# The last rows of a two-layer graph kernel: multiply ahead of the norm, maximum with a negated offset, loads ahead, two store queues

## The chip, the cores and the metric

The kernel runs on one core of a Trainium2 chip. The metric is device time in microseconds, the median of several executions. The span that a profile shows is 1.8 us shorter than the time of the same execution. The profile of the kernel before is of an execution of 2804.74 us, slower than the three timed ones.

In this kernel TensorE does the matmuls, with results in tiles of the memory PSUM; VectorE and ScalarE work on tiles in PSUM or in the other on-chip memory, SBUF, and GpSimd on tiles in SBUF. DMA transfers (loads and stores) are issued from the queues of SyncE and ScalarE, those of the last block before the change all from SyncE. The residual is the `x` that the last step adds.

## The reference, cut to what matters

```python
def _layer_norm(z, a, b, eps=0.001):
    mu = jnp.mean(z, axis=-1, keepdims=True)
    sigma = jnp.std(z, axis=-1, keepdims=True, ddof=1)
    return (z - mu) / (sigma + eps) * a + b
...
for l in range(L):                                  # two layers
    ...                                             # scores, masked exp, attention
    h_lin = jnp.einsum('bsh,oh->bso', h, W_lin[l]) + b_lin[l]
    ctx = jnp.matmul(attention, h_lin)
    h = jax.nn.relu(_layer_norm(ctx, ln_a[l], ln_b[l]))
...
x = x + h                                           # out: 128 x 64 x 768, fp32
```

The mean is already gone in the kernel (the weights are centred), so the norm of a row is one sum of squares. In the data `ln_a` is one and `ln_b` is zero, but the kernel computes both.

## The kernel before

The second layer's second pass goes through 16 blocks `u` of 512 tokens. In the last block it works in two halves `r` of two tiles `k`, 128 rows each. `linear` forms `hl` with 15 groups of matmuls per half, which share the PSUM banks X, Y, Z and V; after each group ScalarE and VectorE add its result into `hl` (`read`). `context` multiplies the attention with `hl` into PSUM tiles `aux`. `finish` does norm, relu and residual:

```python
def finish(u, r):
    cx = context(u, r)
    ...
    for k in range(2):                                              # ScalarE
        nc.scalar.activation(zs[k], cx[k], AF.Square, accum_out=ss[:, k:k + 1])
    nc.scalar.activation(sd, ss, AF.Sqrt, bias=floor, scale=1.0 / (H - 1.0))
    def inverse():                                                  # VectorE
        nc.vector.tensor_scalar_add(rs, sd, EPS_LN)
        nc.vector.reciprocal(rs, rs)
    def scaled(k):
        nc.vector.scalar_tensor_tensor(zs[k], cx[k], rs[:, k:k + 1], rows["a"], op0=ALU.mult, op1=ALU.mult)
        nc.gpsimd.tensor_add(zs[k], zs[k], rows["b"])               # GpSimd
    def done(k):
        nc.vector.scalar_tensor_tensor(xs[k], zs[k], 0.0, xs[k], op0=ALU.max, op1=ALU.add)
        for h in range(PAIR):
            nc.sync.dma_start(out[...], xs[k][h * S:(h + 1) * S])
        if k and (u < NB - 1 or r == 0):
            residual(u + r, 1 - r)                                  # loads the next xs
    return [inverse, scaled(0), scaled(1), done(0), done(1)]        # as closures (cut)
...
linear(u, (0,), 0, {0: ((u - 1, 0), (12, 13, 15, 19, 21)),
                    11: ((u - 1, 1), (34, 35, 36, 42, 44))}, (1,))
linear(u, (1,), 30, {4: ((u, 0), (50, 51, 52, 56, 58))}, ())
for f in finish(u, 1):
    f()
```

The last lines say after which matmul group of the half (0, 11, 4) the earlier rows' context is formed, and in which slots (two per group) its five steps are issued. The trace shows VectorE's instructions in the order of issue: the outputs of slots 56 and 58 start at 2785.10 and 2787.03 us, the sums of Z and V issued behind them at 2786.70 and 2787.90.

## Time and profile before

| what | value | where from |
|---|---|---|
| time | 2802.02 us median of 3 (2799.44 to 2802.55) | runs |
| span, TensorE busy | 2803.0 us, 98% | page |
| last block's first Z matmul to the end | 49.16 us | trace, 2753.80 to 2802.97 |
| of it: to the end of the last sum into `hl` ("E") | 34.51 us | trace |
| from E to the last output add | 9.93 us | trace |
| from the last add to the end | 4.72 us | trace |

TensorE, 98% busy and 94% of the chain on the page, bounds everything up to the last block. After the last V matmuls nothing is left for it but the context, and the end is a chain through VectorE, TensorE, ScalarE, VectorE, GpSimd, VectorE and the stores. The prediction shows that chain line by line. In the lines of a timeline, the columns are start and length in us, engine, line, operation, output<-inputs, shapes and count; in brackets stands the idle time of the engine before it and what ended it. The lengths of neighbours overlap a little.

### The profile page before, as it was taken

How to read it: one execution, taken by the hardware profiler on the slowest of the kernel's cores; microseconds unless marked ns; L12 is line 12 of the kernel's file. 1: busy time of each engine (PE TensorE's matmuls, PEld its weight loads, DVE VectorE, ACT ScalarE, POOL GpSimd, SP SyncE). 2: the span in 40 equal slices, each digit the busy share in tenths (PEclk: the TensorE clock that was granted, in tenths of full speed). 3: DMA queues.
4: the chain of work that ended last, by engine and by line, in shares of the span. 5: the costliest groups of instructions: out<-in, count | busy, mean ns of one | idle time of the engine just before them, and what ended most of it. 6: DMA issues, size and time to landing. Idle time of an engine off the chain costs nothing.

```text
span 2803.0 us, 46102 instructions
## 1 busy us (share of the span) xinstructions
PE 2755.9 (98%) x18712; PEld 2342.4 (84%) x18712; DVE 1340.9 (48%) x2223; ACT 838.7 (30%) x1452; POOL 1190.1 (42%) x935
## 2 busy tenths in 40 slices
PE   7999999999999999999999999999999999999997
PEld 6788888888888888888788888888888888888885
DVE  6454554454544332232345434443444335666666
ACT  2123222322131244444522221212122214545443
POOL 3343333222322556555333353223222335887875
PEclk9999999999999999999999999999999999999999
DMA  5633343234322243343563432343234204555654
GB/s 155 164 78 74 94 115 87 74 88 119 88 74 76 98 141 117 106 130 106 149 160 97 120 79 74 91 119 85 74 85 118 69 25 145 162 169 158 184 162 125
DMA packets 234068, 310.80 MB, mean 111 GB/s; under 512 B 54144, under 2 KB 184448, under 8 KB 225664
## 3 DMA queue, kind: packets, MB, share of 16 engines
q1 hardware_dynamic: 233568, 307.06, 40.0%
q8 instruction: 149, 2.44, 0.4%
q10 hardware_dynamic: 288, 0.79, 0.1%
q14 instruction: 63, 0.52, 0.1%
HBM read 202.91 MB, written 104.86 MB: 110 GB/s over the span
## 4 chain that ended last, share of the span: by engine, by line
PE 94%; DVE 2%; DMA 1%; ACT 1%; issue 1%; SPq 0%; POOL 0%; DVEq 0%; ACTq 0%; POOLq 0%
PE X L366 23%; PE V L366 15%; PE X L637 12%; PE Y L366 11%; PE Z L366 8%; PE V L637 8%; PE Y L637 6%; PE aux L392 5%; PE Z L637 4%; PE aux L564 3%; DVE m L144 1%; DMA ht<-h 0%; DMA h<-xb 0%; ACT ht L255 0%; DVE w_l L144 0%
## 5 line engine op out<-in xcount | busy, mean ns | idle before, releaser
L144 POOL TENSOR_TENSOR ts<-ht 128x512 f32<-128x512 f32 x441 | 585.7, 1340 | 1242.1 <-DMA ht<-h 555.7
L189 ACT ACTIVATE m<-X 128x512 f32<-128x512 f32 x256 | 152.7, 596 | 1117.1 <-PE X L366 589.5
L144 POOL TENSOR_TENSOR ts<-ht,ts 128x512 f32<-128x512 f32 x189 | 248.9, 1325 | 152.8 <-PE X L637 75.9
L144 DVE TENSOR_TENSOR m<-m,V 128x512 f32<-128x512 f32 x256 | 174.4, 681 | 271.9 <-PE V L366 271.9
L144 DVE TENSOR_TENSOR m<-m,X 128x512 f32<-128x512 f32 x256 | 163.8, 682 | 250.2 <-PE X L366 249.5
L366 PE MATMUL X<-ts,w_l 128*128 128x256 f32 x1024 | 246.6, 384 | 6.0 <-DVE w_l L144 2.1
L637 PE MATMUL X<-w_n,ts 128*128 128x256 f32 x1024 | 244.2, 380 | 0.9 <-ACT hl L189 0.6
L366 PE MATMUL X<-ts,w_r 128*128 128x256 f32 x1024 | 242.1, 379 | 0.2 <-ACT m L189 0.2
L144 DVE TENSOR_TENSOR m<-m,Z 128x512 f32<-128x512 f32 x128 | 88.0, 688 | 318.3 <-ACT m L189 257.3
L366 PEld LDWEIGHTS X<-ts,w_l 128*128 128x128 f32 x1024 | 194.2, 192 | 38.5 <-DVE m L144 4.6
L637 PEld LDWEIGHTS X<-w_n,ts 128*128 128x128 f32 x1024 | 191.6, 190 | 32.2 <-DVE hl L144 2.3
L366 PEld LDWEIGHTS X<-ts,w_r 128*128 128x128 f32 x1024 | 192.2, 190 | 29.6 <-ACT m L189 0.6
L255 ACT ACTIVATE ht<-ht,b_col,a_col 128x512 f32<-128x512 f32 x192 | 144.1, 808 | 142.9 <-DMA ht<-h 142.9
L637 PE MATMUL Y<-w_n,ts 128*128 128x256 f32 x768 | 182.4, 379 | 0.0
L366 PE MATMUL Y<-ts,w_l 128*128 128x256 f32 x768 | 181.8, 380 | 0.0
L366 PE MATMUL Y<-ts,w_r 128*128 128x256 f32 x768 | 181.4, 379 | 0.0
L189 ACT ACTIVATE hl<-X 128x512 f32<-128x512 f32 (+1 forms) x136 | 77.9, 573 | 329.4 <-PE X L637 320.0
L366 PEld LDWEIGHTS Y<-ts,w_l 128*128 128x128 f32 x768 | 146.4, 191 | 20.0
L637 PEld LDWEIGHTS Y<-w_n,ts 128*128 128x128 f32 x768 | 145.9, 190 | 19.8
L366 PEld LDWEIGHTS Y<-ts,w_r 128*128 128x128 f32 x768 | 145.9, 190 | 19.8
L603 POOL TENSOR_TENSOR z<-z,b 128x768 f32<-128x768 f32 x64 | 115.4, 1816 | 94.9 <-DVE z L600 94.9
L144 DVE TENSOR_TENSOR hl<-hl,X 128x512 f32<-128x512 f32 (+1 forms) x136 | 83.1, 653 | 147.2 <-PE X L637 139.8
(106 smaller groups left out, 4684.8 us busy)
## 6 DMA issues: line engine op xcount, KB each, us to landing
ht<-h SPq DMA_DIRECT2D x63, 1536.0 KB, 7.2
h<-xb SPq DMA_DIRECT2D x124, 384.0 KB, 6.8
z<-z SPq DMA_DIRECT2D x128, 192.0 KB, 2.9
x<-z SPq DMA_DIRECT2D x128, 192.0 KB, 8.4
xr<-in_x_dram SPq DMA_DIRECT2D x128, 192.0 KB, 3.7
out_dram<-xr SPq DMA_DIRECT2D x128, 192.0 KB, 2.6
x<-in_x_dram SPq DMA_DIRECT2D x120, 192.0 KB, 8.4
adj<-in_adj_dram SPq DMA_DIRECT2D x64, 128.0 KB, 2.8
```

The lines of the kernel that those rows point to most:

```text
L144: (eng.tensor_add if sign == "+" else eng.tensor_sub)(o, a, b)
L189: nc.scalar.activation(to(o), p, AF.Copy, scale=1.0 if sign == "+" else -1.0)
L255: nc.scalar.activation(ht, ht, AF.Relu, bias=cols[1][:, c:c + 1], scale=cols[0][:, c:c + 1])
L366: nc.tensor.matmul(p[:, g], w[ORDER[i][0]][:, c, g * P:(g + 1) * P], b()[t][:, c, :], start=(new and g == c == 0), stop=(c == K2 - 1), ski ...
L392: nc.tensor.matmul(p[h * S + e:h * S + e + 32, q, e:e + 96], ht[:, c, b * S + e:b * S + e + 32], mb[:, e:e + 96], start=(c == 0), stop=(c ...
L564: nc.tensor.matmul(cx[k][i, m, :HH], at[j, q, :], hl[j, q, m * HH:(m + 1) * HH], start=True, stop=True)
L603: nc.gpsimd.tensor_add(zs[k], zs[k], rows["b"])
L637: nc.tensor.matmul(p[:, n], b[t][:, c, r * P:(r + 1) * P], w[s][:, c, :], start=(i in FIRST and i not in PRELOAD and n == c == 0), stop=(c ...
```

## The change

The intent is to shorten the chain after the last matmuls: load residuals earlier, keep VectorE free for the last sums, multiply by `a` before the root is known, replace GpSimd's add and the relu by a maximum (`max(z + b, 0) + x = max(z, -b) + (x + b)`, with `x + b` made ahead), and store through two queues. In the diffs here some reshapes of tiles are left out.

```diff
+            def last_block(u):
+                rest = big.tile([P, C, T], F32, name="ht").rearrange("p c t -> p (c t)")
+                rows["-b"] = sp.tile([P, H], F32, name="nb", bufs=1)
+                ...                                    # XS[u, r]: four slices of rest; load(r): four DMAs
+                put(1, lambda: load(1))
+                put(6, lambda: nc.gpsimd.tensor_scalar_mul(rows["-b"], rows["b"], -1.0))
+                put(20, lambda: load(0))
+                for xs, slot in zip(XS[u, 1], (22, 40)):
+                    put(slot, lambda xs=xs: nc.gpsimd.tensor_add(xs, xs, rows["b"]))
+
+            def finish_last(u, r):
+                ...
+                for k in (1, 0):
+                    nc.scalar.activation(squares[:, k], cx[k], AF.Square, accum_out=ss[k])
+                    nc.vector.tensor_tensor(zs[1 - k], cx[1 - k], rows["a"], op=ALU.mult)
+                    nc.scalar.activation(rs[k], ss[k], AF.Sqrt, bias=floor, scale=1.0 / (H - 1.0))
+                for k in (1, 0):
+                    nc.vector.tensor_scalar_add(rs[k], rs[k], EPS_LN)
+                    nc.vector.reciprocal(rs[k], rs[k])
+                    nc.vector.scalar_tensor_tensor(zs[k], zs[k], rs[k], rows["-b"], op0=ALU.mult, op1=ALU.max)
+                    nc.vector.tensor_add(xs[k], xs[k], zs[k])
+                    for h, queue in enumerate((nc.sync, nc.scalar)):
+                        queue.dma_start(out[u * NBB + batch(r, k, h)], xs[k][h * S:(h + 1) * S])
...
-                        if k and (u < NB - 1 or r == 0):
+                        if k and u + r < NB - 1:
...
-                    linear(u, (0,), 0, {0: ..., 11: ((u - 1, 1), (34, 35, 36, 42, 44))}, (1,))
-                    linear(u, (1,), 30, {4: ((u, 0), (50, 51, 52, 56, 58))}, ())
+                    # in the last layer:
+                    linear(u, (0,), 0, {0: ..., 9: ((u - 1, 1), (28, 29, 30, 39, 41))}, (1,))
+                    linear(u, (1,), 30, {2: ((u, 0), (44, 45, 47, 61, 62))}, ())
-                    for f in finish(u, 1):
+                    for f in (finish_last if last else finish)(u, 1):
```

More of the change, by code (lines that the diff above doesn't have):

```diff
@@ L571, in pass_two, with load @@
             XS = {}
+            def last_block(u):
+                rest = big.tile([P, C, T], F32, name="ht").rearrange("p c t -> p (c t)")
+                rows["-b"] = sp.tile([P, H], F32, name="nb", bufs=1)
+                for r in range(2):
+                    XS[u, r] = [rest[:, n * H:(n + 1) * H] for n in (2 * r, 2 * r + 1)]
+                def load(r):
+                    for k in range(2):
+                        for h in range(PAIR):
+                            nc.sync.dma_start(XS[u, r][k][h * S:(h + 1) * S], x[u * NBB + batch(r, k, h)])
+                put(1, lambda: load(1))
[4 more added lines that the diff above has]
+            def finish_last(u, r):
+                cx = context(u, r)
+                zs = [sp.tile([P, H], F32, name="z", bufs=4) for _ in range(2)]
+                squares = sp.tile([P, Q, H], F32, name="hl", bufs=2)
+                two = "p (n d) -> p n d"
+                xs = XS[u, r]
+                ss = [stat.tile([P, 1], F32, name="ss_e", bufs=2) for _ in range(2)]
+                rs = [stat.tile([P, 1], F32, name="sd_e", bufs=2) for _ in range(2)]
+                for k in (1, 0):
+                    nc.scalar.activation(squares[:, k].rearrange(two, n=2), cx[k], AF.Square, accum_out=ss[k])
+                    nc.vector.tensor_tensor(zs[1 - k].rearrange(two, n=2), cx[1 - k],
+                                            rows["a"].rearrange(two, n=2), op=ALU.mult)
+                    nc.scalar.activation(rs[k], ss[k], AF.Sqrt, bias=floor, scale=1.0 / (H - 1.0))
[6 more added lines that the diff above has]
+                        queue.dma_start(out[u * NBB + batch(r, k, h)], xs[k][h * S:(h + 1) * S])
+                return []
             def residual(u, r):
@@ L676, in pass_two @@
                         put_sums_t((1, 1, 0), 38, 2, 30)
-                    linear(u, (0,), 0, {0: ((u - 1, 0), (12, 13, 15, 19, 21)),
-                                        11: ((u - 1, 1), (34, 35, 36, 42, 44))}, (1,))
-                    linear(u, (1,), 30, {4: ((u, 0), (50, 51, 52, 56, 58))}, ())
+                        ends = ({0: ((u - 1, 0), (12, 13, 15, 19, 21)), 11: ((u - 1, 1), (34, 35, 36, 42, 44))},
+                                {4: ((u, 0), (50, 51, 52, 56, 58))})
+                    else:
+                        last_block(u)
+                        ends = ({0: ((u - 1, 0), (12, 13, 15, 19, 21)), 9: ((u - 1, 1), (28, 29, 30, 39, 41))},
+                                {2: ((u, 0), (44, 45, 47, 61, 62))})
+                    linear(u, (0,), 0, ends[0], (1,))
+                    linear(u, (1,), 30, ends[1], ())
                     for n in sorted(plan):
                         run(n)
-                    for f in finish(u, 1):
+                    for f in (finish_last if last else finish)(u, 1):
                         f()
```

## The prediction

> **What bounds the kernel now.** I read the page's busy shares and its chain of waits first.
>
> ```profile
> PE 2755.9 (98%) x18712; PEld 2342.4 (84%) x18712; DVE 1340.9 (48%) x2223; ACT 838.7 (30%) x1452; POOL 1190.1 (42%) x935
> ...
> PE 94%; DVE 2%; DMA 1%; ACT 1%; issue 1%; SPq 0%; POOL 0%; DVEq 0%; ACTq 0%; POOLq 0%
> ```
>
> TensorE carries 94% of the chain, and the diff touches no matmul. What it touches is the last of 16 blocks of the second layer, some 50 us of 2803, and within these the stretch after the last matmuls. So I read the timeline of the last 23 us next (start us, us, engine, line, operation, count, then idle time before and its releaser).
>
> ```profile
> 2781.24 1.94 DVE L600 SCALAR_TENSOR_TENSOR z<-aux,rs,a 128x768 f32<-128x768 f32 x2
> ...
> 2783.89 1.13 PE L637 MATMUL V<-w_n,ts 128*128 128x256 f32 x4 [0.84 <-DVE hl L144]
> ...
> 2785.10 1.68 DVE L615 SCALAR_TENSOR_TENSOR xr<-z,xr 128x768 f32<-128x768 f32 x1 [1.27 <-DMA xr<-in_x_dram]
> 2786.70 0.41 DVE L144 TENSOR_TENSOR hl<-hl,Z 128x256 f32<-128x256 f32 x1
> ...
> 2787.03 0.95 DVE L615 SCALAR_TENSOR_TENSOR xr<-z,xr 128x768 f32<-128x768 f32 x1
> ...
> 2787.90 0.41 DVE L144 TENSOR_TENSOR hl<-hl,V 128x256 f32<-128x256 f32 x1
> ...
> 2788.37 1.50 PE L564 MATMUL aux<-hl,at 64*64 64x384 f32 x10 [0.34 <-DVE hl L144]
> ...
> 2789.30 0.81 ACT L590 ACTIVATE z<-aux 128x768 f32<-128x768 f32 x1 [11.32 <-PE aux L564]
> ```
>
> The last V matmul ends at 2785.02, but its sum into hl (L144) ends only at 2788.31: VectorE first waits for a residual load, then does the outputs of the rows before (L615) ahead of the last two sums. Call the end of that sum E. The context matmuls and the whole tail hang on it. The rest of the same timeline:
>
> ```profile
> 2791.84 1.94 DVE L600 SCALAR_TENSOR_TENSOR z<-aux,rs,a 128x768 f32<-128x768 f32 x2
> 2793.00 3.56 POOL L603 TENSOR_TENSOR z<-z,b 128x768 f32<-128x768 f32 x2 [7.03 <-DVE z L600]
> 2794.84 3.41 DVE L615 SCALAR_TENSOR_TENSOR xr<-z,xr 128x768 f32<-128x768 f32 x2 [1.05 <-POOL z L603]
> 2797.40 2.42 SPq L617 DMA_DIRECT2D out_dram<-xr  x4
> ```
>
> After E: context matmuls, two squares, one root, reciprocal, two scalings, the offset on GpSimd, two outputs, four stores one behind the other.
>
> A narrow window of VectorE shows why its two outputs take 3.41 us: the first of them alone. Below it, the timeline of GpSimd and VectorE 20 to 30 us earlier:
>
> ```profile
> 2794.84 2.54 DVE L615 SCALAR_TENSOR_TENSOR xr<-z,xr 128x768 f32<-128x768 f32 x1 [1.05 <-POOL z L603]
> ```
>
> ```profile
> 2760.51 3.58 POOL L603 TENSOR_TENSOR z<-z,b 128x768 f32<-128x768 f32 x2 [2.37 <-DVE z L600]
> ...
> 2762.84 2.07 DVE L615 SCALAR_TENSOR_TENSOR xr<-z,xr 128x768 f32<-128x768 f32 x1
> ```
>
> The output op takes 0.95 us alone, but 2.54 or 2.07 when GpSimd is in an add: it ends 0.82 us after GpSimd's add does (2796.56 and 2797.38; 2764.09 and 2764.91). It is shut out, not slowed.
>
> [...] L144 and L600, which take one input from PSUM, keep 0.41 and 1.01 us beside GpSimd. [...] L615 measures 945 to 953. The new multiply, max and add get 0.95 us each (0.93 apart when pipelined without a wait, as the L600 pair shows). [...] Here four issues take 2.42 us on SyncE, and a store lands 2.7 us (median 2.8) after its issue.
>
> **The change, part by part.** I walked the queues by hand on the clock of the profile before, with its durations (TensorE group 0.87 us apart, L144 0.42, GpSimd add of 768 1.80, square with its accumulator 0.90, root 0.30, the two small ops on rs 0.45 together).
>
> *A, residuals and slots ahead of the end.* Contexts and scalings move two to four matmul groups earlier; the outputs of rows (u,0) move behind the last sums; their residual is loaded one half-block earlier. This takes away: the context's wait for PSUM (its 16 matmuls took 2.17 us at 2772.59, against 1.52 elsewhere: 0.65), the 0.84 us wait of the last V matmuls (two L600 sat in front of the sum that they need), and the block of 1.27 + 1.68 + 0.95 us before the last sums. With nothing in its place, V would end at about 2783.6 and E be 2784.05, 4.26 us earlier.
>
> *B, what comes in its place.* The two new GpSimd adds of the offset (1.80 us each) read SBUF and fall beside VectorE outputs. First: GpSimd ends the two L603 at 2764.09, VectorE's waiting output goes to 2764.91, the new add takes 2764.8 to 2766.6, the second output is shut out until then and ends at 2767.43, a microsecond later than before (2766.44). The sum of V behind it ends at about 2768.1, and the V matmuls that share its bank start there instead of 2767.2: 0.9 us lost on TensorE. Second: GpSimd's L603 pair for (u-1,1) ends at about 2774.2, the new add at 2776.0, the first output (ready 2774.6) ends at 2776.85, the second at 2778.07; then the reciprocal and the first scaling reach 2779.45, the two sums of X end at 2780.1 and X's next matmuls, due at 2779.3, start there: 0.85 us lost. The rest runs free: V from 2783.75 to 2784.8, E = 2785.25. So A and B together give 2788.31 - 2785.25 = 3.06 us.
>
> *C, the tail after E.* VectorE becomes its chain. Outputs of (u,0): two, to 2787.0. (The context ends at E + 1.6 = 2786.85, just before.) Multiply tile 0 while ScalarE squares tile 1 (2786.87 to 2787.77, root 2788.1); multiply tile 1 to 2788.83; ScalarE squares tile 0 meanwhile, root by 2789.3. Then for tile 1: rs 0.4, max 0.95 after a 0.1 us wait on rs, add 0.95, to 2791.2; the same for tile 0, to 2793.55. From E that is 8.3 us; before it was 2798.24 - 2788.31 = 9.93. Gone are GpSimd's 1.8 us and the exclusion of 1.6 us, added are four more VectorE passes over 768. Gain 1.63.
>
> *D, two store queues.* Before, the last add ends at 2798.24, the fourth store is issued at 2799.28, the program ends at 2802.97: 4.73 us. Now the last two stores are issued together at once, so the fourth's 1.04 us goes. [...] from the trace's 0.6 us between issues, I give back half of it. Gain 0.7.
>
> Sum: 3.06 + 1.63 + 0.7 = 5.4 us, 0.2%. From 2802.02 that makes 2796.6.
>
> **The rivals.** (i) The offset adds do not collide ([...] the residual lands late enough): E comes 1.2 us sooner and the time is 2795.4. For it: the load of these rows is issued only at about 2759.5, behind four stores and four loads on SyncE, and loads here land 2.6 to 4.9 us later, so the exact start of the first add is a guess. Against it: the second collision doesn't depend on that. (ii) The collisions cost more, or the residual of (u-1,1), now behind four more loads on SyncE's queue, comes late: I have it landing at 2774.2 to 2776.3, and needed at 2774.6 and 2777. VectorE would then hold up V and X for another 2 us: 2798.6. (iii) The tail gains nothing since the last store's landing dominates: the 2.7 us landing is in my sum as untouched, so that can only be true of part D: 2797.3. (iv) A slower tail because each engine waits for the other's tile: the waits are met within 0.1 us in C, and the second half of VectorE's chain waits for no one, so at most 0.5 us more. (v) The main body moves: 2750 us of it is the same instructions, but the three runs before differ by 3.1 us, more than half of the effect.
>
> **Range and chances.** Walk errors of about 1.5 us either way, and about 1.5 us of run-to-run spread, give 2793.6 to 2799.8. A change of 2% is 56 us; the whole stretch that the diff touches is about 50, so within 2% is all but certain.
>
> **What would show it.** In the profile after: the last sum hl<-hl,V ends directly behind its matmuls (within 0.5 us, not 3.3), about 3 us sooner from the start than before; one or two TensorE waits of 0.8 to 1 us on hl or X in the last two half-blocks, beside a GpSimd add of b; from E to the last add 8.3 us with VectorE without a gap above 0.3 us; no GpSimd work after E; stores from SyncE and ScalarE starting together, and the end 3.7 to 4.3 us after the last add. It is wrong if a residual load or TensorE waits over 1.5 us show up in the last block, if the tail from E to the end exceeds 13 us, or if the time differs by over 4 us from 2796.6 in runs of the same session.

Part B rests on the outputs that ended 0.82 us after GpSimd's adds, and C on the 0.95 us of L615. In D 1.04 less half of the 0.6 us between two issues makes the 0.7; that half is the author's estimate. The 2.6 to 4.9 us in (i) are of loads and stores together; the loads alone, from 2750 us to the end of the kernel before, landed 3.4 to 4.9 us after their issue.

## The result, and the profile after

The changed kernel took 2791.8 us median (2790.55 to 2793.72, 4 runs), against 2800.99 us for the kernel before (2799.44 to 2802.55, 4 runs). The ratio is 0.9968, 95% interval 0.9951 to 0.9985. Ratios here are the mean of one kernel's runs over that of the other's of the same rounds, so not quite the ratio of the medians. The gain in the medians is 9.2 us, where 5.4 were predicted, and 2791.8 lies below the range.

The page of the changed kernel, busy shares and chain, is as before: TensorE carries 94%.

```profile
PE 2749.5 (99%) x18712; PEld 2339.4 (84%) x18712; DVE 1341.5 (48%) x2227; ACT 837.5 (30%) x1453; POOL 1192.8 (43%) x936
...
PE 94%; DVE 2%; issue 1%; DMA 1%; POOL 1%; ACT 1%; SPq 0%; ACTq 0%; DVEq 0%; POOLq 0%
```

Its timeline from the last matmuls on:

```profile
2776.76 1.03 PE L680 MATMUL V<-w_n,ts 128*128 128x256 f32 x4
...
2777.72 2.08 PE L564 MATMUL aux<-hl,at 64*64 64x384 f32 x16
2777.83 0.42 DVE L144 TENSOR_TENSOR hl<-hl,V 128x256 f32<-128x256 f32 x1 [0.44 <-PE V L680]
2778.16 1.82 DVE L658 SCALAR_TENSOR_TENSOR ht<-z,ht 128x768 f32<-128x768 f32 x2
...
2779.84 0.81 ACT L603 ACTIVATE hl<-aux 128x768 f32<-128x768 f32 x1 [8.61 <-PE aux L564]
2779.90 1.83 DVE L604 TENSOR_TENSOR z<-aux,a 128x768 f32<-128x768 f32 x2
...
2782.03 1.02 DVE L610 SCALAR_TENSOR_TENSOR z<-z,sd_e,nb 128x768 f32<-128x768 f32 x1
2783.08 0.96 DVE L611 TENSOR_TENSOR ht<-ht,z 128x768 f32<-128x768 f32 x1
...
2784.06 2.78 SPq L613 DMA_DIRECT2D out_dram<-ht  x2
2784.07 2.81 ACTq L613 DMA_DIRECT2D out_dram<-ht  x2
...
2785.39 0.96 DVE L611 TENSOR_TENSOR ht<-ht,z 128x768 f32<-128x768 f32 x1
```

The last sum now follows its matmuls at once (E = 2778.25), the outputs of the earlier rows come behind it and cost 1.82 us in place of 2.6 and more, VectorE runs from E to the last add with no gap above 0.1 us, and GpSimd has no work left. The last two stores start together (0.01 us apart). Before E, the walk of the prediction looked for two collisions with GpSimd. Both places are in this cut of the same timeline:

```profile
2759.40 0.94 DVE L658 SCALAR_TENSOR_TENSOR xr<-z,xr 128x768 f32<-128x768 f32 x1
...
2759.80 2.21 POOL L590 TENSOR_TENSOR ht<-ht,b 128x768 f32<-128x768 f32 x1 [1.80 <-DMA ht<-in_x_dram]
...
2761.41 0.63 DVE L638 TENSOR_SCALAR rs<-sd 128x2 f32<-128x2 f32 x1
...
2767.33 1.81 POOL L590 TENSOR_TENSOR ht<-ht,b 128x768 f32<-128x768 f32 x1
...
2769.00 0.96 DVE L658 SCALAR_TENSOR_TENSOR xr<-z,xr 128x768 f32<-128x768 f32 x1 [1.12 <-DMA xr<-in_x_dram]
...
2773.20 1.13 PE L680 MATMUL X<-w_n,ts 128*128 128x256 f32 x4 [0.67 <-DVE hl L144]
```

The first GpSimd add came later than predicted, as it waited for its load. VectorE's output had already started, so this time GpSimd was shut out (2.21 us for an add of 1.8), and only the small op on `rs` behind it was held (0.63 us for 0.16). At the second place the add was there as predicted, but VectorE was recorded waiting for a residual load. Yet its output ended at 2769.96, 0.82 us after the add (2769.14), and that distance is the mark of a blocked output in the prediction; so both may have held it. TensorE lost 0.67 us on X.

Put side by side, the last block and the rest:

| us | before | after | gain | predicted |
|---|---|---|---|---|
| first Z matmul of the last block at | 2753.80 | 2747.70 | 6.1 | 0 |
| from there to E | 34.51 | 30.55 | 3.96 | 3.06 |
| E to the last add | 9.93 | 8.09 | 1.84 | 1.63 |
| last add to the end | 4.72 | 4.09 | 0.63 | 0.7 |
| sum of the last block | 49.16 | 42.74 | 6.42 | 5.4 |

Between these two profiles only half of the difference of 12.5 us lies where the change is. (It is larger than that of the medians because the profiled execution of the kernel before was a slow one, 2804.74 us against 2800.99.) The other half is there before the first changed instruction. I paired the 18712 matmuls of both traces in their order: the later one is 2.8 us ahead after 37 matmuls, 4.3 us after the first 100 us of the span, 6.1 us at the last block, and the steps are few. Two views of windows show the large ones. The columns are the window and its length, then busy us (instructions) by engine, the granted TensorE clock, the DMA share and GB/s. Kernel before:

```profile
22.00:27.00 5.00, 5.00 (x15) 4.03 (x14) 3.35 (x6) 0.60 (x1) 0.00 (x0) 1.00 1.01 276
```

```profile
88.00:99.00 11.00, 7.90 (x27) 6.20 (x24) 2.92 (x7) 1.98 (x4) 7.80 (x8) 0.69 0.74 241
```

Kernel after:

```profile
22.00:27.00 5.00, 5.00 (x25) 4.39 (x24) 4.89 (x9) 1.79 (x3) 0.00 (x0) 1.00 1.02 274
```

```profile
88.00:99.00 11.00, 9.76 (x37) 8.31 (x38) 4.07 (x11) 3.43 (x6) 5.01 (x5) 0.84 0.46 156
```

In the same 5 us of full business TensorE did 15 matmuls in one execution and 25 in the other. By their start times they come 0.43 us apart in the kernel before until 26.1 us, and 0.22 us apart in the other from 20.7 us on: half the rate for longer. (The clock printed for this window is 1.00 in both, so it doesn't show the difference. 0.43 us is also the spacing where 0.50 is printed: in the kernel before, 8 matmuls of this shape took 3.62 us from 93.88 us, with 0.50 from 94 to 96 us. That the clock was that low before 26.1 us too is inference.) Around 90 us the granted clock is 0.69 against 0.84. The instructions are the same. The question for the experiments was whether this belongs to the change or to the execution, and what the parts of the last block are worth.

### The profile page after: what moved, and what is told of

It is laid out like the page before. It is cut to its first block, busy times and chain, and to the rows that moved or that the text cites. A ratio compares the mean times of both kernels' runs of the same rounds, so it can differ in the third digit from the quotient of the medians.

```text
span 2790.4 us, 46097 instructions
## 1 busy us (share of the span) xinstructions
PE 2749.5 (99%) x18712; PEld 2339.4 (84%) x18712; DVE 1341.5 (48%) x2227; ACT 837.5 (30%) x1453; POOL 1192.8 (43%) x936
## 4 chain that ended last, share of the span: by engine, by line
PE 94%; DVE 2%; issue 1%; DMA 1%; POOL 1%; ACT 1%; SPq 0%; ACTq 0%; DVEq 0%; POOLq 0%
PE X L366 23%; PE V L366 15%; PE X L680 12%; PE Y L366 11%; PE Z L366 8%; PE V L680 8%; PE Y L680 6%; PE aux L392 5%; PE Z L680 4%; PE aux L564 3%; POOL w_r L144 1%; DVE m L144 0%; DMA z<-z 0%; DVE w_l L144 0%; DVE wm L406 0%
## 5 line engine op out<-in xcount | busy, mean ns | idle before, releaser
L144 DVE TENSOR_TENSOR hl<-hl,V 128x512 f32<-128x512 f32 (+1 forms) x136 | 89.0, 655 | 128.2 <-PE V L680 127.7
```

Source lines behind the costliest of these rows:

```text
L144: (eng.tensor_add if sign == "+" else eng.tensor_sub)(o, a, b)
```

## The experiments

Nine runs, three of them of unchanged code, each with five rounds against fresh runs of the kernel before; all gave correct results. A job is a session that measures several kernels in turn: the first four runs below are of one job on chip 12, the next three and the last two of two jobs on chip 8. The record names no chip for the first measurement, so job and chip are not separated. "Block" is the time from the last block's first Z matmul to the end of the span. Means are of the runs of one job.

### The kernel before, again

No edit.

> The kernel before, unchanged, as a null. The measured gain of the change was 9.2 us in the medians and 12.5 us between the two profiles, of which only 6.4 us lie in the last block (the block's first matmuls start 6.1 us earlier already). Theory 1 (the 6.1 us are the granted clock of these two executions: a 0.5 stage of 6.8 us against 3.4 us, and a later rise to full clock at the start): the ratio here is 1.000 within 0.001, and the start of the last block in this profile lies anywhere between 2747 and 2754 us. Theory 2 (the change really makes the first 2750 us faster, for example by where its instructions lie): this kernel's last block starts at 2753 to 2754 us in every execution, and kernels with changed tails at about 2748.

Measured: 2801.92 us median (2798.52 to 2803.68), before 2800.68 (9 runs), ratio 1.0006 (0.9993 to 1.0019). The block took 49.16 us again, to the hundredth, but started at 2751.16 instead of 2753.80. So the body of the unchanged kernel wanders by microseconds while the block does not. That fits theory 1, though one start inside the expected range doesn't exclude theory 2.

### Loads and slots alone

```diff
-                    for f in (finish_last if last else finish)(u, 1):
+                    for f in finish(u, 1):
     # and without "-b" and the two gpsimd.tensor_add of last_block
```

> Only the loads ahead of time and the new slots; the old tail with GpSimd's offset and one store queue. From the walk of the profile after: the last sum into hl should end 30.3 to 30.6 us after the last block's first Z matmul (before 34.5), so 3.9 to 4.2 us of gain; from there to the end about 14.5 us as before. If the local account is right: 2797 (ratio 0.9986) when the body is equal. Theory 2 of the null (body faster in changed kernels): about 2794.5.

Measured: 2797.14 us median (2795.43 to 2799.19), ratio 0.9992 (0.9978 to 1.0005). E at 30.26 us in the block, the tail 14.73, the block 44.99: 4.17 us of gain from part A (4.25 at E), with nothing taken back by GpSimd's adds of the offset, which are not there. The X matmuls still lost 0.39 us here, as VectorE waited 0.59 us for the same residual load. The median is the 2797 of the local account, not the 2794.5 of theory 2. The block started at 2750.03. The old tail's exclusion is unchanged, as this line shows, the same 3.41 us as before:

```profile
2786.91 3.41 DVE L654 SCALAR_TENSOR_TENSOR ht<-z,ht 128x768 f32<-128x768 f32 x2 [1.06 <-POOL z L642]
```

### The new tail with the old slots

```diff
-   9: ((u - 1, 1), (28, 29, 30, 39, 41))        2: ((u, 0), (44, 45, 47, 61, 62))
+  11: ((u - 1, 1), (34, 35, 36, 42, 44))        4: ((u, 0), (50, 51, 52, 56, 58))
```

> The new tail and the loads ahead, with the slots of before. The last sum should again end late, 34 to 34.5 us after the block's first Z matmul, since two outputs sit in front of it, but the tail then starts without two outputs in front of it: about 11 us from the last sum to the end against 14.7 before and 12.2 after. Gain 3.5 to 4 us, 2797.3 (ratio 0.9987) by the local account; about 2794.5 by the theory that changed kernels have a faster body.

Measured: 2800.05 us median (2794.43 to 2800.32), ratio 0.9995 (0.9983 to 1.0008). The block took 47.54 us, a gain of 1.62, less than half of what I expected, and both numbers of the expectation were off. E came at 35.36, 0.85 us later than in the kernel before, and the tail from E to the end took 12.18, the same as in the changed kernel, which has the two outputs in it. Two cuts of the timeline say why:

```profile
2773.02 1.82 POOL L590 TENSOR_TENSOR ht<-ht,b 128x768 f32<-128x768 f32 x1
...
2773.33 3.19 DVE L658 SCALAR_TENSOR_TENSOR xr<-z,xr 128x768 f32<-128x768 f32 x2
...
2777.24 1.13 PE L680 MATMUL X<-w_n,ts 128*128 128x256 f32 x4 [0.90 <-DVE hl L144]
...
2788.74 0.96 DVE L604 TENSOR_TENSOR z<-aux,a 128x768 f32<-128x768 f32 x1 [0.59 <-ACT hl L603]
```

VectorE's two outputs took 3.19 us beside GpSimd's second add of the offset, where they took 1.82 us in the kernel before, and the X matmuls lost 0.90 us: the collision that the prediction described, in full. In the last line VectorE stands idle for 0.59 us before the multiply of tile 1, and the trace puts that down to ScalarE's square of that tile (L603). So the tail is bound twice: context, square of tile 1 and second multiply end at E + 3.48, and two outputs, two multiplies end at E + 3.48 as well. Putting the outputs behind the last sum was free in the tail (12.18 us without them, 12.19 with them).

### The second residual load later

```diff
-                put(20, lambda: load(0))
+                put(44, lambda: load(0))
```

> The changed kernel with one load moved: the residual of rows (u,0) is issued at slot 44 instead of 20, so that the residual of (u-1,1) no longer waits behind it on SyncE's queue. In the profile after, VectorE waited 1.12 us for that residual and the X matmuls then 0.67 us for VectorE. My recorded step B put that stall down to the second GpSimd add (0.85 us). If the residual is the cause: the 1.12 us wait and the 0.67 us stall are gone and the last sum ends 0.6 to 0.7 us sooner in the block (29.9 us after its first Z matmul). If GpSimd's add is the cause: the stall stays, 0 us.

Measured: 2792.06 us median (2791.59 to 2796.4), ratio 0.9975 (0.9962 to 0.9987); E at 30.54, the block 42.86. The stall stayed, but not for the reason that the profile of the changed kernel gives:

```profile
2767.04 1.80 POOL L590 TENSOR_TENSOR ht<-ht,b 128x768 f32<-128x768 f32 x1
...
2767.51 2.15 DVE L658 SCALAR_TENSOR_TENSOR xr<-z,xr 128x768 f32<-128x768 f32 x1
...
2772.91 1.13 PE L680 MATMUL X<-w_n,ts 128*128 128x256 f32 x4 [0.66 <-DVE hl L144]
```

The wait for the residual is gone, and the same output is now shut out by GpSimd's add for as long: 2.15 us in place of 0.95, with its end again 0.82 us after the add's. The two causes lay on top of each other, and the profile of the changed kernel names only one of them.

### The changed kernel, again

> The changed kernel again, unchanged, beside fresh runs of the kernel before. In all six profiles so far the time from the last block's first Z matmul to the end is fixed by the kernel (before 49.16 twice, after 42.74: 6.4 us apart), while that first matmul comes anywhere from 2747.4 to 2753.8 us, with the stages of half clock in the first 100 us. Theory 1 (the rest of the 9.2 us was the luck of four executions): block to end 42.7 again, a gain near 6.4 us in the means, the median at 2794.2. Theory 2 (the change makes the body faster): about 9 us again, median at 2791.5, and its block starts before 2749.

Measured: 2795.68 us median (2793.21 to 2797.34), before 2802.19 (2798.99 to 2804.98, 9 runs), ratio 0.9976 (0.9962 to 0.9989). In the means 2795.46 against 2802.04: 6.6 us. The block took 42.74 us again and started at 2751.87, 4.2 us later than in the first profile of the same code and later than in the second profile of the kernel before. So a start wanders by that much between executions, and the 6.1 us of the first pair of profiles need no effect of the change. The block and the means are as theory 1 has them. That the granted clock is the whole cause, as theory 1 says, is not shown.

### One queue for the last four stores

```diff
-                    for h, queue in enumerate((nc.sync, nc.scalar)):
+                    for h, queue in enumerate((nc.sync, nc.sync)):
```

> The changed kernel with its last four stores all issued from SyncE. Recorded step D gives 0.7 us to the two queues together with the stores of the first tile being out of the way; measured from the last add to the end are 4.72 us before and 4.09 after. If the second queue is what saves it: 4.6 to 4.7 us here. If it is the order of the tiles (two of four stores issued 2.3 us earlier)[...]: 4.1 to 4.3 us. The rest of the block as in the changed kernel: 38.6 us from the first Z matmul to the last add.

Measured: 2795.2 us median (2793.25 to 2796.03), ratio 0.9975 (0.9962 to 0.9987). From the last add to the end 4.03 us, against 4.09 with two queues. The second queue is worth nothing here. What pays, by exclusion, is that tile 1's two stores are issued 2.3 us before tile 0's (0.9 us lay between the two in the kernel before), so the last two find the queue free (with one queue, the first two are issued from 2787.94 us and the last two from 2790.25, and no issue took over 0.6 us). No run keeps this tail and stores all four at the end.

```profile
2787.94 3.42 SPq L613 DMA_DIRECT2D out_dram<-ht  x4
```

Four issues over 3.42 us, the pairs apart; the last two, one behind the other, end as early as two side by side.

### GpSimd's adds moved, and the load after the residual

```diff
-                put(20, lambda: load(0))
-                for xs, slot in zip(XS[u, 1], (22, 40)):
-                    put(slot, lambda xs=xs: nc.gpsimd.tensor_add(xs, xs, rows["b"]))
+                put(24, lambda: load(0))
+                put(49, lambda: nc.gpsimd.tensor_add(XS[u, 1][1], XS[u, 1][1], rows["b"]))
+                def offset():                       # the copy holds GpSimd until the outputs of (u, 0) are done
+                    t = stat.tile([P, 1], F32, name="hold", bufs=1)
+                    nc.gpsimd.tensor_copy(t, XS[u, 0][1][:, :1])
+                    nc.gpsimd.tensor_add(XS[u, 1][0], XS[u, 1][0], rows["b"])
+                put(63, offset)
```

> The changed kernel with the second residual load issued after that of (u-1,1), and with GpSimd's two adds of the offset moved: one behind its last add for (u,0), one held back until the outputs of (u,0) are done, so that it lies beside the multiplies from PSUM. Removing the residual wait alone (e5) changed nothing in the block, since GpSimd's add then shut out the same output for as long. If those two together are the cause of the stalls of TensorE (0.28 and 0.67 us): both are gone here, the last sum ends 29.6 us after the block's first Z matmul (30.55 in the changed kernel), the tail stays 12.2, block to end 41.8 us. If something else holds VectorE there, 42.7 us as before. A collision of the held add with the first max would show as that max taking over 1.1 us.

Measured: 2793.32 us median (2791.9 to 2795.01), before 2802.19, ratio 0.997 (0.9957 to 0.9982); in the means 8.55 us below the kernel before and 2.0 below the changed kernel of the same job. The block took 42.26 us, half a microsecond less than the changed kernel and half more than I had expected: E at 29.92.

```profile
2774.17 1.13 PE L686 MATMUL X<-w_n,ts 128*128 128x256 f32 x4
...
2780.87 1.83 DVE L610 TENSOR_TENSOR z<-aux,a 128x768 f32<-128x768 f32 x2
...
2781.15 1.81 POOL L594 TENSOR_TENSOR ht<-ht,b 128x768 f32<-128x768 f32 x1
```

No wait is marked at X any more (its group still starts 1.08 us after the group before, where 0.87 is the usual step), and GpSimd's add lies beside multiplies that read PSUM and slows them by nothing (1.83 us for the two, as without it). The tail is 0.15 us longer (12.34), the last adds starting 0.1 us after the maxima in place of 0.03. This kernel is the fastest of those tried in its block; of the 2.0 us in the means only the block's 0.5 can be credited to it.

### The changed kernel, a third time, and with the multiply late

> The changed kernel a third time, unchanged, in another session. Two sessions of it gave means 9.0 us (4 runs each) and 6.6 us (5 and 9 runs) below the kernel before, while its last block took 42.74 us both times. If the gain is the block's 6.4 us and the rest is the start of the block wandering: a difference of means between 5 and 8 us, and the block 42.7 us again. If the change speeds the body up: 8 us or more.

Measured: 2794.41 us median (2793.12 to 2798.16), before 2800.91 (9 runs), ratio 0.998 (0.9966 to 0.9993); in the means 6.2 us. The block took 42.76 us.

```diff
-                    nc.vector.tensor_tensor(zs[1 - k], cx[1 - k], rows["a"], op=ALU.mult)       # in the first loop
-                    nc.vector.scalar_tensor_tensor(zs[k], zs[k], rs[k], rows["-b"], op0=ALU.mult, op1=ALU.max)
+                    nc.vector.scalar_tensor_tensor(zs[k], cx[k], rs[k], rows["a"], op0=ALU.mult, op1=ALU.mult)
+                    nc.vector.tensor_tensor(zs[k], zs[k], rows["-b"], op=ALU.max)
```

> The changed kernel without the multiply ahead: the tile is multiplied by rs and the scale in one instruction once rs is known, then maximum and add, so VectorE has the same three passes of 768 for each tile but waits while ScalarE squares. If VectorE is the chain of the tail, as recorded step C has it, the last add ends about 9.6 us after the last sum into hl (two outputs to 1.75, then waiting for the first root at 2.85, then two times 3.4) instead of 8.1: 1.5 us more in the block, 44.2 us from the first Z matmul to the end. If the overlap is worth nothing because the stores or the squares end last: 8.1 and 42.7.

Measured: 2794.49 us median (2793.97 to 2796.81), ratio 0.9978 (0.9965 to 0.999). The last add ended 9.62 us after E and the block took 44.59 us (0.34 us of the difference to 42.74 lies before E). VectorE waits where the changed kernel multiplies:

```profile
2782.14 0.15 DVE L606 TENSOR_SCALAR sd_e<-sd_e 128x1 f32<-128x1 f32 x1 [1.12 <-ACT sd_e L604]
...
2787.95 0.96 DVE L611 TENSOR_TENSOR ht<-ht,z 128x768 f32<-128x768 f32 x1
```

So the multiply beside the square is worth 1.5 us, as forecast. The run times of this kernel and of the changed one in the same job (means 2794.9 and 2795.1) do not show it, and that is a useful warning: 1.8 us in the block drown in the wandering of its start.

## Why the prediction was right or wrong

**The time was outside the range, and the step that failed is the last one**, "about 1.5 us of run-to-run spread". I took the spread of single runs of the kernel before as if it were the whole of it and started from its median of three. The same code of the changed kernel gave medians of 2791.8, 2795.68 and 2794.41 us in three jobs, 3.9 us apart, and single runs from 2790.55 to 2798.16, with the block the same to 0.02 us. Of the 4.8 us between 2796.6 and 2791.8, 1.0 is the starting value (2802.02 for 2800.99), 1.0 the block (6.4 us for 5.4), and the other 2.8 us lie outside the part that was changed. By themselves the block's 1.0 us would have stayed inside the range. The prediction's own sign of being wrong, over 4 us from 2796.6, came true. Of the other two, the tail stayed under 13 us (12.2), and a wait of over 1.5 us for a residual load came on GpSimd alone (1.80 us; VectorE's was 1.12, TensorE's longest 0.67).

Over all jobs the mean is 2794.3 us (14 runs) against 2801.2 us for the kernel before (36 runs): a gain of 6.9 us, with a standard error of 0.7 if the runs are taken as independent, which agrees with the 6.4 us of the block. Less the block and the 1.8 us outside the span, these means put the block's start at 2749.8 us with the change and 2750.2 without, 0.4 us apart, less than the error. The rest of the 9.2 us of the first four runs I put down to luck; that something of that session had a part in it is not excluded. Rival (v), "the main body moves", named this and I gave it too little width.

Where the body wanders can be read from all eleven profiles. Matmul 1000 starts between 167.1 and 172.9 us and the block between 2747.4 and 2753.8, in nearly the same order (correlation 0.89), while the stretch between the two varies by 3.3 us. So most of it is settled in the first 170 us. The granted clock from 80 to 100 us is 0.83 in both profiles of the kernel before; in three profiles of the same changed code it is 0.91, 0.91 and 1.00. It differs between executions of one kernel, then, but it is not the whole: loads and slots alone had 1.00 there and only 15 matmuls between 22 and 27 us. What decides these stages stays open, and so do the small steps after 100 us, which I didn't trace.

**Part A was right in its mechanism.** The last sum follows its matmuls (0.46 us, not 3.3), the context of (u,0) takes 1.52 us again, and loads and slots alone bring E 4.25 us sooner, where the step had 4.26. That the two agree so closely is partly luck: the 4.25 contain a residual wait that cost 0.39 us on X, and with that wait and the collisions gone E comes 4.59 us sooner (34.51 to 29.92).

**Part B was too large: 1.2 us of collisions predicted, 0.3 measured.** (E is at 30.26 us in the block without GpSimd's adds and at 30.55 with them.) This is what separates 3.06 from 3.96. The first collision had been put at 0.9 us and cost nothing. The add's load landed 1.8 us into GpSimd's idle time, so VectorE's output came first. V started 1.15 us after Z in place of the usual 0.87, but it did so too with loads and slots alone, where that add doesn't exist. That is the uncertainty which rival (i) named ("the exact start of the first add is a guess"). The second stall was put at 0.85 us and measured 0.67, but the profile gives another reason, the residual that rival (ii) had feared. The experiments show that both reasons are real: take away the residual wait and the collision fills the place; with the old slots the collision alone costs 0.90 us. With both gone, E is 0.6 us sooner. So the 0.3 us are what the adds cost on top of the residual wait; without that wait they cost 0.6 (30.54 against 29.92). Not everything beside an add of GpSimd was held: the small tensor_scalar on two columns took 0.63 us in place of 0.16 there in the changed kernel, that on one column 0.14 us with the adds moved. The sum has a slip besides: its stalls of 0.9 and 0.85 us add to 1.75, its result takes 1.2 for them and doesn't say why.

**Part C was right to 0.2 us** (8.09 for 8.3; and 9.62 for the 9.6 that the last experiment expected without the multiply ahead), but its account of the first 3.5 us was incomplete. I had VectorE's two outputs as the chain; the experiment with the old slots shows that context, square and second multiply end at the same moment. Of the passes over 768 that I put at 0.95 us each, the multiply from PSUM (L604) took 0.95 to 0.96 in the changed kernel, the add from SBUF (L611) 0.96 and the maximum (L610) 1.02. L610 is a scalar_tensor_tensor with a scalar per row, as L643 is (1.01 to 1.02), and the outputs L658, with a constant, took 0.95 where they were not blocked; their operations differ too, so that the scalar is the cause is not shown.

**Part D had the right sum (0.63 for 0.7) and the wrong reason, which is luck.** The term that I credited, the fourth store's 1.04 us of issue less the 0.3 us that I estimated to come back, was put down to the two queues. With one queue the end came as early. By exclusion the gain is that of storing tile 1 while tile 0 is still computed.

## What to carry to other kernels

Time a small change at the end of a long kernel by the length of its own stretch in the trace, from a fixed instruction to the end, and repeat both kernels, unchanged, in several jobs before believing a difference of a few microseconds. When a wait goes away and the stall stays, look for a second cause that ended just before the first: here GpSimd's add (2.15 us in place of 0.95) and a residual load (a wait of 1.12 us) held the same instruction. In a kernel like this one, try to keep GpSimd's SBUF work beside VectorE instructions that read PSUM (here two multiplies took 1.83 us beside its add, as without it, and two outputs on SBUF 3.19 in place of 1.82), and store finished tiles as they come before thinking of more queues (from the last add to the end 4.03 us with one queue and 4.09 with two).
